# Order of work in a two-layer attention and expert kernel: paired copies and spreads of x's sums, gathered rows turned behind pieces, attention's first units in another order

## The chip, the cores and the metric

The kernel runs on one core of a Trainium2 chip. A core has a matrix engine (TensorE, called PE here; PEld is its weight load), VectorE (DVE), ScalarE (ACT), GpSimd (POOL) and SyncE (SP, which only issues transfers here), each with its own instruction stream in program order. They meet through semaphores. Matrix products go to PSUM, banks of 2 KB on each of 128 partitions; everything else lives in SBUF. The metric is device time in microseconds (us), lower is better.

## The reference

x is 8 batches of 256 tokens with 256 features, in float32. Four blocks follow one another, each added to x:

```python
x = x + L0_xattn(layernorm(x), ctx, ctx)   # autocorrelation attention: one row per batch, added to all tokens
x = x + L0_ffn(layernorm(x))               # 8 experts, each gets exactly 256 tokens
x = x + L1_xattn(layernorm(x), ctx)        # 16 heads of 16, softmax attention
x = x + L1_ffn(layernorm(x))               # top 2 of 8 experts, and a shared one
```

The parts that this change touches are the end of the first block, the second, and the beginning of the third:

```python
# L0_ffn
norm = layer_norm(feat);  scores = norm @ centroids.T
for e in range(8):                       # balanced: each expert takes its best C = 256 of the tokens left
    idx_e = top_k(where(taken, -inf, scores[:, e]), C);  taken[idx_e] = True
routed = feat[idx];  h = layer_norm(routed)
out = routed + gelu(h @ w1 + b1) @ w2 + b2     # per expert, put back in place
# L1_xattn
q = norm(x) @ Wq;  k, v = ctx @ Wkv;  out = softmax(q k / 4) v @ Wp
```

## The kernel before

All of it is one program in which the order of instructions on each engine is written out by hand: an engine runs what is emitted for it in just that order. The function is `fast_path`.

**x's sums (L1848 to L2128).** After the first block each batch b needs x plus a row of its own. `copy_rows(b)` multiplies x of a batch by the identity into a PSUM tile `po`; `spread_rows(b)` adds the batch's row of PB to it, on one of four groups of 32 rows of the array (group b // 2). `order_b` is 0, 2, 4, 6, 1, 3, 5, 7, so neighbours in it lie on different groups. `take(b)` computes mean and variance from `po` on DVE (`tile_stats`, two a batch), copies it back to X on ACT and stores it to NMd in DRAM. For two batches `act_sums` gets the sums on ACT instead, with `squares` behind it. `factors` (rstd by pow on POOL and a Newton step), `widen` and `factor_rows` turn the factors to rows `psr` on PE; `factors_out` copies them to `srow`; `times_factors` multiplies the scores `ps0` (expert 0) and `psx` (all) by them to `n0` and SC. Before that, `pw` and `pb` are small products copied to WCn and `bound`, `pr3` and `pp` give PB, and `pcp` gives cP, which `rows_part` adds to the scores. The PSUM pools are `ps_t` (four banks), `ps_k` (two) and one bank for the tag `pg`.

**The search (L2179 to L2535).** For experts 0 to 6 in turn, `search` finds the score limit in five rounds: DVE counts scores above a trial limit, PE sums the counts (`pcn`, L2210), DVE makes the next trial. While an expert is searched for, the list of the one before is built, a step a round (`list_tokens`: pse, ppl, `pid`, pix, then the gather of its 256 rows from NMd into R, issued by POOL). Between `pcn`s PE runs pieces from a queue called `work`: each piece is one 0.43 us matmul of a longer computation (keys and values of the third block, then the products of the experts). `fill(us)` takes pieces for that many us by their assumed costs. `start_ffn` calls `ffn` for the expert whose rows were gathered; it is called in round r == 1 of a search, after the first search, and in the tail. `ffn` has ACT scale R, PE transpose it at once (`prt`, L2378), ACT copy it to RT (L2382), and puts its products (`ph`, then `py`) at the end of `work`. More than 24 pieces in the queue are run before a new `ffn`:

```python
        if listed:
            while len(work) > 2 * NF + 8:
                work.popleft()[1]()
            ffn(*listed.popleft())
```

**Attention's start (L2544 to L3060).** The experts' results come back from DRAM (Yd) as `yg`; `add_y` adds them to X on DVE. For each batch `batch_stats` (DVE, pow on POOL, a Newton step of four operations on POOL or DVE), `norm_q` (h), `turn_q` (transposes `pt`, L2622) and `queries` (QM, half on ACT, half on DVE) come before its `scores` (`p`, L2669; exponentials on ACT) and `values` (`pv`). Values of the context tiles from EARLY on are pieces of `work`; those before it are computed here by `vals`. The main loop goes over units (batch b, half c of the heads).

Of the kernel before, what the change touches and what calls it, by code (L numbers as in the profile page):

```python
# [1086 lines left out]
def fast_path(  # L1087
# [276 lines left out]
    kmax = pk.tile([P, NB, NTB], F32, name="kmax")  # L1364


    EARLY = 7

    def attention_columns():

# [477 lines left out]
    def rows_of(b):  # L1848
        return X[:, TPB * b : TPB * (b + 1), :]

    def copy_rows(b, pool):
        pos[b] = pool.tile(
            [P, TPB, D], F32, tag="pt" if pool is ps_t else "pm", name="po"
        )
        nc.tensor.matmul(
            pos[b].rearrange("p h d -> p (h d)"),
            ident,
            rows_of(b).rearrange("p h d -> p (h d)"),
            start=True,
            stop=False,  # L1860
            skip_group_check=True,
        )
# [13 lines left out]
            )  # L1876

    for b in order_b[:4]:
        copy_rows(b, ps_t)
    fill(0.87)  # L1880
    WCn = pa.tile([P, 3, 32], F32, name="WCn")
    pw = ps_a.tile([P, 3, 32], F32, tag="pg", name="pw")
    for j in range(3):
        for dc in range(KC):
            nc.tensor.matmul(
# [3 lines left out]
                start=(dc == 0),  # L1889
                stop=(dc == KC - 1),  # L1890
            )
    nc.vector.tensor_copy(WCn, pw)
    bnd = pa.tile([E, 1], F32, name="bnd")
    nc.vector.tensor_scalar(bnd, cs[:, 1:2], 1.01, None, ALU.mult)
    bdiag = pa.tile([E, E], F32, name="bdiag")
    nc.vector.tensor_scalar(bdiag, ident[:E, :E], bnd, None, ALU.mult)
    pb = ps_k.tile([P, E], F32, tag="pm", name="pb")
    nc.tensor.matmul(pb, ones[:E, :], bdiag, start=True, stop=True)
# [39 lines left out]
    pcp = ps_k.tile([P, 32], F32, tag="pm", name="pcp")  # L1938
    for j in range(2):
        nc.tensor.matmul(  # L1940
            pcp, R3[:, j, :], WCn[:, j, :], start=(j == 0), stop=(j == 1)
        )
    PB = pa.tile([P, D], F32, name="PB")
    nc.vector.tensor_tensor(PB, pp, boutb, ALU.add)
    cP = pa.tile([P, 32], F32, name="cP")
    nc.vector.tensor_tensor(cP, pcp, WCn[:, 2, :], ALU.add)

    rm = pa.tile([P, NT, 2], F32, name="rm")
    r2, mr2 = rm[:, :, 0], rm[:, :, 1]
# [12 lines left out]
            )  # L1962


    psr = ps_a.tile([P, 2, TPB, P], F32, tag="pg", name="psr")

    def factor_rows(k):
        for h in range(TPB):
# [58 lines left out]
    def factors(q0, q1, eng):  # L2027
        qs = slice(q0, q1)
        return rstd(MV[:, qs, :], r2[:, qs], 1.0 + LN_EPS, LN_EPS**2, eng, mr2[:, qs])
# [16 lines left out]
        nc.vector.tensor_tensor(dst[:, halves[m]], ps[:, halves[m]], srow[:, m, :], ALU.mult)  # L2046

    def factors_out(m):
        nc.scalar.copy(srow[:, m, :], psr[:, m].rearrange("p h t -> p (h t)"))

    b = order_b
    spread_rows(*b[:4])
    copy_rows(b[4], ps_k)
    squares = act_sums(b[3])
    take(b[:1])
    squares()
    spread_rows(b[4])
    copy_rows(b[5], ps_t)
    spread_rows(b[5])
    take(b[1:2])  # L2060
    squares = act_sums(b[5])
    take(b[2:3])
    newton_a, means_a = factors(0, 8, nc.gpsimd)
    newton_a()
    squares()
    for i in b[6:]:
        copy_rows(i, ps_t)
        spread_rows(i)

    def rows_part(ps, cols):  # L2070

# [12 lines left out]
            )  # L2084

    rows_part(ps0, cP[:, 0:1].to_broadcast([P, 32]))
    take(b[4:5])
    widen(0, 8, nc.scalar)
    newton_2, means_2 = factors(8, 12, nc.gpsimd)
    factor_rows(0)  # L2090
# [15 lines left out]
    means_2()  # L2106
    means_3(nc.gpsimd)
    store_factors(1)
    nc.scalar.copy(sx1, psx[:, halves[1]])
    factors_out(1)  # L2110
    times_factors(n0, ps0, 1)
    nc.gpsimd.tensor_tensor(SC[:, halves[1]], sx1, srow[:, 1, :], ALU.mult)
    next(columns)
    pb1 = ps_t.tile([P, E * NF], F32, tag="pt", name="pb1")
    nc.tensor.transpose(pb1, b1r, ident[: E * NF, : E * NF])
    b1c = pr.tile([P, E, NF], F32, name="b1c")
    nc.vector.tensor_copy(b1c.rearrange("p e f -> p (e f)"), pb1)

# [3 lines left out]
    for r in range(NCT):  # L2122
        psel = ps_t.tile([16, P], F32, tag="pt", name="psel")
        nc.tensor.transpose(psel, a16[:, r, :], ident)
        nc.vector.tensor_copy(rowsel[:, r, :], psel)

    ac.close()
    acp.close()  # L2128
# [223 lines left out]
    def ffn(e, ids, R):  # L2352
# [7 lines left out]
        prt = ps_t.tile([P, KC, NCT, P], F32, tag="pt", name="prt")  # L2360
        for r in range(NCT):
            nc.scalar.activation(
                R[:, r, 0:D],
                R[:, r, 0:D],
                AF.Identity,
                bias=R[:, r, D + 1 :],
                scale=R[:, r, D : D + 1],
            )
            if e in TPART and r == NCT - 1:

                nc.scalar.copy(blank[:, D : D + 1], blank[:, D + 1 : D + 2])
                n0_, n1_ = TPART[e]
                nc.sync.dma_start(
                    out=Td.rearrange("(n p) w -> p n w", p=P)[:, n0_:n1_, :],
                    in_=blank.unsqueeze(1).to_broadcast([P, n1_ - n0_, ROW]),
                )
            for kc in range(KC):
                nc.tensor.transpose(  # L2378
                    prt[:, kc, r, :], R[:, r, kc * P : (kc + 1) * P], ident
                )  # L2380
        for kc in range(KC):
            nc.scalar.activation(  # L2382
                RT[:, kc, :],
                prt[:, kc].rearrange("p r q -> p (r q)"),
                AF.Identity,
                bias=gbc[:, 1, kc : kc + 1],
                scale=gbc[:, 0, kc : kc + 1],
            )

        def up(f):  # L2390
            ph = ps_h.tile([P, CAP], F32, tag="ph", name="ph")
# [160 lines left out]
    py = ct_scope.enter_context(tc.tile_pool(name="py", bufs=2, side="right"))  # L2552
    warm = small.tile([P, 1], F32, tag="warm", name="warm")
    nc.scalar.activation(warm, ones[:, 0:1], AF.Exp)
    ygs = [py.tile([P, NF, D], F32, tag="yg", name="yg") for _ in range(2)]
    for i0, i1 in ((2, 4), (4, 8), (8, 16)):
        nc.sync.dma_start(
            out=ygs[i0 // 8][:, i0 % 8 : (i1 - 1) % 8 + 1, :],
            in_=Yd.rearrange("(c p) d -> p c d", p=P)[:, i0:i1, :],
        )  # L2560

    QM, hTs, h2s, norms = {}, {}, {}, {}

    def add_y(i, n):

        nc.vector.tensor_tensor(
            X[:, i : i + n, :],
            X[:, i : i + n, :],
            ygs[i // 8][:, i % 8 : i % 8 + n, :],
            ALU.add,  # L2570
        )

    def batch_stats(b, tag, eng=nc.gpsimd):

# [400 lines left out]
    for b in range(B):  # L2975
        for c in range(NB):
# [489 lines left out]
```

## Time and profile before

| | |
|---|---|
| median of three runs | 902.32 us (894.98 to 902.54) |
| the profiled execution | 899.05 us, of which the instructions span 897.3 |
| busy in that span | PE 866.9, DVE 307.1, ACT 266.7, POOL 217.3 us |
| sums of x and the start of the search (45 to 67) | PE busy 20.49 of 22 us, DVE 15.61 |
| search (60 to 185) | PE busy 113.60 of 125 us |
| last two experts (185 to 231) | PE busy 42.67 of 46 us |
| start of attention (231 to 262) | PE busy 27.90 of 31 us |
| rest, from 400 on | PE busy 491.71 of 497 us |

Busy is the time in which an engine had at least one instruction running. A wait row of the profile names the instruction that waited, what released it, and how long the engine stood idle for it. The granted clock is the share of PE's full clock that the chip allowed in a stretch; at 0.50 the same matmul takes about twice as long. In a timeline row, "x8" joins eight instructions, and a float32 product here is two of them.

### The profile page before, as it was taken

Reading aid. Unit: us, or ns where it says so; the run is one execution under the profiler, and the core shown is the slowest. Engines: PE = TensorE matmul, PEld = TensorE weight load, DVE = VectorE, ACT = ScalarE, POOL = GpSimd, SP = SyncE. Lnnn points to the kernel's source line nnn. Section 1 sums busy time; section 2 is a strip of 40 time slices with the busy share of each in tenths; the row PEclk is TensorE's granted clock in tenths of the full one; section 3 lists DMA queues with packets and bytes.
Section 4 is the critical chain, followed back from the end, with each engine's and each line's share of the span. In section 5 each row is a group of like instructions: output and inputs, shape, how many; then the busy total and the mean of one; then the engine's idle time right before and its main releaser. Section 6 shows DMA issues by size and latency. Waiting matters only on the chain.

```text
span 897.3 us, 11174 instructions
## 1 busy us (share of the span) xinstructions
PE 866.9 (97%) x4200; PEld 539.0 (60%) x4200; DVE 307.1 (34%) x1016; ACT 266.7 (30%) x499; POOL 217.3 (24%) x302
## 2 busy tenths in 40 slices
PE   8999888989999999999999999999999999999997
PEld 7546677778745555544748565656565556574745
DVE  7377865330445575454112111111111111111011
ACT  4255453224377677431010111111111111111110
POOL 7060221221335554433320011020202131111200
PEclk9999999999999999999999999999999999999999
DMA  7564379642250001081120535555555633311130
GB/s 244 185 201 162 117 218 277 189 136 82 94 141 2 1 1 37 20 312 54 66 68 24 188 100 155 174 154 176 143 186 134 193 88 110 88 12 13 14 104 27
DMA packets 86218, 105.21 MB, mean 117 GB/s; under 512 B 7915, under 2 KB 76748, under 8 KB 86124
## 3 DMA queue, kind: packets, MB, share of 16 engines
q1 hardware_dynamic: 77642, 91.09, 31.7%
q0 software_dynamic: 7920, 13.02, 6.8%
q8 instruction: 35, 0.57, 0.2%
q10 hardware_dynamic: 594, 0.30, 0.1%
q14 instruction: 27, 0.22, 0.1%
HBM read 80.60 MB, written 25.37 MB: 118 GB/s over the span
## 4 chain that ended last, share of the span: by engine, by line
PE 84%; DMA 4%; DVE 3%; issue 3%; POOL 2%; ACT 2%; ACTq 0%; POOLq 0%; DVEq 0%; SPq 0%
PE pgt L3086 19%; PE py L3108 18%; PE pu L3086 18%; PE py L2410 6%; PE ph L2393 4%; PE p L2669 4%; PE pv L2684 3%; DMA R<-NMd,ids 2%; PE pp L2735 2%; PE pp L2636 1%; PE pp L1406 1%; PE pgu L3281 1%; PE pt L2622 1%; DMA C<-in_ctx_dram 1%; PE pt L3142 1%
## 5 line engine op out<-in xcount | busy, mean ns | idle before, releaser
L3095 DVE TENSOR_TENSOR A<-A,pu 128x512 f32<-128x512 f32 x96 | 66.0, 688 | 365.2 <-PE pu L3086 358.5
L3094 ACT ACTIVATE A<-pgt 128x512 f32<-128x512 f32 x96 | 57.4, 598 | 271.4 <-PE pgt L3086 271.4
L3155 POOL DMA_INDIRECT Od<-Y,ids x32 | 49.5, 1546 | 303.5 <-ACT Y L3168 208.6
L3086 PE MATMUL pgt<-RT,wa 128*128 128x512 f32 x256 | 121.1, 595 | 0.0
L3086 PE MATMUL pu<-RT,wb 128*128 128x512 f32 x256 | 120.3, 592 | 0.0
L3108 PE MATMUL py<-wc,A 128*128 128x256 f32 x512 | 111.8, 379 | 0.0
L3108 PEld LDWEIGHTS py<-wc,A 128*128 128x128 f32 x512 | 96.7, 190 | 13.3 <-issue 0.5
L2677 ACT ACTIVATE ex<-p,scale 128x512 f32<-128x512 f32 x128 | 77.5, 691 | 33.7 <-PE p L2669 33.7
L3086 PEld LDWEIGHTS pu<-RT,wb 128*128 128x128 f32 x256 | 48.6, 190 | 61.2 <-issue 60.0
L3086 PEld LDWEIGHTS pgt<-RT,wa 128*128 128x128 f32 x256 | 47.6, 190 | 54.9 <-issue 54.5
L2393 PE MATMUL ph<-RT,w 128*128 128x256 f32 x256 | 63.7, 398 | 0.2 <-ACT A L2402 0.2
L2410 PE MATMUL py<-w,A 128*128 128x256 f32 x256 | 60.3, 385 | 0.0
L2393 PEld LDWEIGHTS ph<-RT,w 128*128 128x128 f32 x256 | 47.7, 198 | 9.4 <-ACT A L2402 1.8
L2402 ACT ACTIVATE A<-ph,b1c 128x256 f32<-128x256 f32 x64 | 30.2, 474 | 75.2 <-PE ph L2393 73.4
L2410 PEld LDWEIGHTS py<-w,A 128*128 128x128 f32 x256 | 47.3, 190 | 6.4
L2909 POOL DMA_INDIRECT Td<-HP,to x32 | 31.6, 988 | 64.6 <-DMA Td<-HP,to 61.5
L3086 PE MATMUL pgt<-HT,wa_-1_2777 128*128 128x512 f32 x96 | 45.5, 596 | 0.0
L3086 PE MATMUL pu<-HT,wb_-1_2778 128*128 128x512 f32 x96 | 45.1, 592 | 0.0
L2669 PE MATMUL p<-QM,KT 32*128 32x512 f32 x256 | 44.6, 651 | 0.4 <-DVE QM L2650 0.4
L3168 ACT ACTIVATE Y<-py,R 128x256 f32<-128x256 f32 x32 | 15.2, 474 | 96.5 <-PE py L3108 96.5
L3108 PE MATMUL py<-wc_-1_2779,A 128*128 128x256 f32 x192 | 41.9, 379 | 0.0
L3108 PEld LDWEIGHTS py<-wc_-1_2779,A 128*128 128x128 f32 x192 | 36.4, 190 | 5.8 <-issue 1.0
(463 smaller groups left out, 1001.6 us busy)
## 6 DMA issues: line engine op xcount, KB each, us to landing
w<-in_L_ffn_w_dram SPq DMA_DIRECT2D x16, 1024.0 KB, 5.6
wa<-in_L_ffn_w_e_dram SPq DMA_DIRECT2D x8, 1024.0 KB, 5.5
wb<-in_L_ffn_w_e_dram SPq DMA_DIRECT2D x8, 1024.0 KB
wc<-in_L_ffn_w_e_dram SPq DMA_DIRECT2D x8, 1024.0 KB
R<-Td SPq DMA_DIRECT2D x8, 530.0 KB
sa<-in_L_ffn_w_e_dram SPq DMA_DIRECT2D x16, 256.0 KB, 3.9
sb<-in_L_ffn_w_e_dram SPq DMA_DIRECT2D x16, 256.0 KB, 6.2
sc<-in_L_ffn_w_e_dram SPq DMA_DIRECT2D x16, 256.0 KB, 2.9
```

The costliest lines, as they stand in the source:

```text
L2393: nc.tensor.matmul(ph, w1[:, kc, f * P : (f + 1) * P], RT[:, kc, :], start=(kc == 0), stop=(kc == KC - 1),)
L2402: nc.scalar.activation(A[:, f, :], ph, AF.Gelu_apprx_tanh, bias=b1c[:, e, f : f + 1])
L2410: nc.tensor.matmul(py, A[:, f, r * P : (r + 1) * P], w2[:, f, :], start=(f == 0), stop=(f == NF - 1),)
L2669: nc.tensor.matmul(ps[g].rearrange("p m q -> p (m q)"), KT[rows, c, k0 : k0 + P], QM[b][rows, c].rearrange("p m q -> p (m q)"), start=True ...
L2677: nc.scalar.activation(e4[:, g], ps[g], AF.Exp, scale=scale)
L2684: nc.tensor.matmul(pvs[b, c][32 * g : 32 * g + 32, m, :], VA[:, b * TPB + kt, 8 * c + 2 * g + m, :], ex[b, c, kt][:, g, m, :], start=(kt = ...
L2909: nc.gpsimd.indirect_dma_start(out=Td, out_offset=bass.IndirectOffsetOnAxis(ap=to[g][:, k, j : j + 1], axis=0), in_=HP[:, GT * g + j, :], ...
L3086: nc.tensor.matmul(ps, w_[:, kc, fs], xs[kc], start=(kc == 0), stop=(kc == KC - 1),)
L3094: nc.scalar.activation(a, pgt, AF.Silu)
L3095: nc.vector.tensor_tensor(a, a, pu, ALU.mult)
L3108: nc.tensor.matmul(py, A[:, f, s : s + P], wc[:, f, :], start=(f == 0), stop=(f == NF - 1))
L3155: nc.gpsimd.indirect_dma_start(out=Od, out_offset=bass.IndirectOffsetOnAxis(ap=ids, axis=0), in_=Y, in_offset=None, compute_op=ALU.add,)
```

## The change

In x's sums, the fifth batch's copy takes the place of two pieces, the last four batches are copied and spread as two pairs, `act_sums` is left to one batch, `pb` shares the bank of `pw` and comes first, `pcp` is computed later, `psr` is allocated at its first use, `srow` is copied ahead of `sx1`, and three small copies go from DVE to ACT:

```diff
-    EARLY = 7
+    EARLY = 6
...
     for b in order_b[:4]:
-        copy_rows(b, ps_t)
-    fill(0.87)
+        copy_rows(b, ps_t, "pt")
+    copy_rows(order_b[4], ps_k, "pm")
+    bnd = pa.tile([E, 1], F32, name="bnd")
+    nc.vector.tensor_scalar(bnd, cs[:, 1:2], 1.01, None, ALU.mult)
+    bdiag = pa.tile([E, E], F32, name="bdiag")
+    nc.vector.tensor_scalar(bdiag, ident[:E, :E], bnd, None, ALU.mult)
     WCn = pa.tile([P, 3, 32], F32, name="WCn")
-    pw = ps_a.tile([P, 3, 32], F32, tag="pg", name="pw")
+    pw = ps_a.tile([P, 4, 32], F32, tag="pg", name="pw")
+    pb = pw[:, 3, 0:E]
+    nc.tensor.matmul(pb, ones[:E, :], bdiag, start=True, stop=True)
...
     spread_rows(*b[:4])
-    copy_rows(b[4], ps_k)
+    copy_rows(b[5], ps_a, "pg")
+    spread_rows(*b[4:6])
     squares = act_sums(b[3])
     take(b[:1])
     squares()
-    spread_rows(b[4])
-    copy_rows(b[5], ps_t)
-    spread_rows(b[5])
     take(b[1:2])
-    squares = act_sums(b[5])
+    pcp = ps_t.tile([P, 32], F32, tag="pt", name="pcp")
+    for j in range(2):
+        nc.tensor.matmul(
+            pcp, R3[:, j, :], WCn[:, j, :], start=(j == 0), stop=(j == 1)
+        )
+    for i in b[6:]:
+        copy_rows(i, ps_t, "pt")
+    spread_rows(*b[6:])
     take(b[2:3])
+    cP = pa.tile([P, 32], F32, name="cP")
+    nc.vector.tensor_tensor(cP, pcp, WCn[:, 2, :], ALU.add)
     newton_a, means_a = factors(0, 8, nc.gpsimd)
     newton_a()
-    squares()
-    for i in b[6:]:
-        copy_rows(i, ps_t)
-        spread_rows(i)
...
-    take(b[4:5])
+    take(b[4:6])
...
+    factors_out(1)
     nc.scalar.copy(sx1, psx[:, halves[1]])
-    factors_out(1)
...
-    nc.vector.tensor_copy(b1c.rearrange("p e f -> p (e f)"), pb1)
+    nc.scalar.copy(b1c.rearrange("p e f -> p (e f)"), pb1)
...
-        nc.vector.tensor_copy(rowsel[:, r, :], psel)
+        nc.scalar.copy(rowsel[:, r, :], psel)
```

In the search, the transposes of an expert's rows and the copy to RT become an entry of `work`, charged 0.5 us, behind up to three entries that are there; and `start_ffn` is called in round 2 instead of 1:

```diff
+        def turn_rows():
+            prt = ps_t.tile([P, KC, NCT, P], F32, tag="pt", name="prt")
+            for r in range(NCT):
+                for kc in range(KC):
+                    nc.tensor.transpose(
+                        prt[:, kc, r, :], R[:, r, kc * P : (kc + 1) * P], ident
+                    )
             for kc in range(KC):
...
+                nc.scalar.activation(
+                    RT[:, kc, :],
...
+        work.insert(min(3, len(work)), (0.5, turn_rows))
...
-            if r == 1 and e >= 2:
+            if r == 2 and e >= 2:
                 start_ffn()
```

At attention's start, Y is loaded batch by batch into two buffers, each load two batches ahead, and added batch by batch; batch 1's Newton step and all of its normalization are DVE's; both halves of batch 0's queries come before the first scores, and the values of tiles 4 and 5 behind them:

```diff
+    def load_y(b):
+        if b < B:
+            ygs[b] = py.tile([P, TPB, D], F32, tag="yg", name="yg")
+            nc.sync.dma_start(
+                out=ygs[b],
+                in_=Yd.rearrange("(c p) d -> p c d", p=P)[:, TPB * b : TPB * (b + 1), :],
+            )
+
+    load_y(1)
+    load_y(2)
...
+    def add_y(b):
+        xb = X[:, TPB * b : TPB * (b + 1), :]
+        nc.vector.tensor_tensor(xb, xb, ygs.pop(b), ALU.add)
+        load_y(b + 2)
...
-    add_y(TPB, TPB)
-    batch_stats(1, "q")
+    add_y(1)
+    batch_stats(1, "q", nc.vector)
     queries(0, 0)
-    norm_q(1, nc.gpsimd, nc.vector)
+    queries(0, 1)
+    norm_q(1, nc.vector, nc.vector)
     add_bias(0)
     add_bias(1)
-    list(vals(4, 1, ps_m))
...
             if prev is None:
-                queries(0, 1)
+                list(vals(4, 1, ps_m, nc.vector.tensor_copy))
                 turn_q(1)
-                add_y(4, 4)
-                list(vals(5, 2, ps_m, nc.vector.tensor_copy))
+                add_y(2)
+                batch_stats(2, "q")
...
-                if b + 2 < B:
+                if b + 2 < B and b:
+                    add_y(b + 2)
                     batch_stats(b + 2, "q")
...
             if prev is None:
-                add_y(8, 4)
-                add_y(12, 4)
+                list(vals(5, 1, ps_m, nc.vector.tensor_copy))
                 ct_scope.close()
```

More of the change, by code (lines that the diff above doesn't have):

```diff
@@ L1849, in rows_of, with copy_rows @@
         return X[:, TPB * b : TPB * (b + 1), :]
[L1851 to L1854, printed above, removed]
+    def copy_rows(b, pool, tag):
+        pos[b] = pool.tile([P, TPB, D], F32, tag=tag, name="po")
         nc.tensor.matmul(
@@ L1891, in fast_path @@
             )
[L1892 to L1898, printed above, removed]
+    nc.vector.tensor_copy(WCn, pw[:, 0:3, :])
     bound = pr.tile([P, E], F32, name="bound")
@@ L1937, in fast_path @@
         nc.tensor.matmul(pp, R3[:, j, :], woutr[:, j, :], start=(j == 0), stop=(j == 1))
[L1938 to L1942, printed above, removed]
     PB = pa.tile([P, D], F32, name="PB")
     nc.vector.tensor_tensor(PB, pp, boutb, ALU.add)
-    cP = pa.tile([P, 32], F32, name="cP")
-    nc.vector.tensor_tensor(cP, pcp, WCn[:, 2, :], ALU.add)
     rm = pa.tile([P, NT, 2], F32, name="rm")
@@ L1962, in store_factors @@
             )
-    psr = ps_a.tile([P, 2, TPB, P], F32, tag="pg", name="psr")
+    psrs = []
     def factor_rows(k):
+        if k == 0:
+            psrs.append(ps_a.tile([P, 2, TPB, P], F32, tag="pg", name="psr"))
+        psr = psrs[0]
         for h in range(TPB):
@@ L2048, in factors_out @@
     def factors_out(m):
-        nc.scalar.copy(srow[:, m, :], psr[:, m].rearrange("p h t -> p (h t)"))
+        nc.scalar.copy(srow[:, m, :], psrs[0][:, m].rearrange("p h t -> p (h t)"))
     b = order_b
     spread_rows(*b[:4])
-    copy_rows(b[4], ps_k)
+    copy_rows(b[5], ps_a, "pg")
+    spread_rows(*b[4:6])
     squares = act_sums(b[3])
@@ L2359, in ffn @@
         Y = pf.tile([P, NCT, D], F32, tag="Y", name="Y")
-        prt = ps_t.tile([P, KC, NCT, P], F32, tag="pt", name="prt")
         for r in range(NCT):
@@ L2376, in ffn @@
                 )
-            for kc in range(KC):
-                nc.tensor.transpose(
-                    prt[:, kc, r, :], R[:, r, kc * P : (kc + 1) * P], ident
-                )
[L2381 to L2388, printed above, removed]
+        def turn_rows():
[5 more added lines that the diff above has]
+                    )
+            for kc in range(KC):
+                nc.scalar.activation(
+                    RT[:, kc, :],
+                    prt[:, kc].rearrange("p r q -> p (r q)"),
+                    AF.Identity,
+                    bias=gbc[:, 1, kc : kc + 1],
+                    scale=gbc[:, 0, kc : kc + 1],
+                )
+        work.insert(min(3, len(work)), (0.5, turn_rows))
         def up(f):
@@ L2551, in fast_path @@
     pq2 = at.enter_context(tc.tile_pool(name="pq2", bufs=2))
-    py = ct_scope.enter_context(tc.tile_pool(name="py", bufs=2, side="right"))
+    py = at.enter_context(tc.tile_pool(name="py", bufs=2))
     warm = small.tile([P, 1], F32, tag="warm", name="warm")
     nc.scalar.activation(warm, ones[:, 0:1], AF.Exp)
[L2555 to L2560, printed above, removed]
-    QM, hTs, h2s, norms = {}, {}, {}, {}
[L2564 to L2571, printed above, removed]
+    ygs = {}
+    def load_y(b):
[7 more added lines that the diff above has]
+    load_y(2)
+    QM, hTs, h2s, norms = {}, {}, {}, {}
+    def add_y(b):
+        xb = X[:, TPB * b : TPB * (b + 1), :]
+        nc.vector.tensor_tensor(xb, xb, ygs.pop(b), ALU.add)
+        load_y(b + 2)
     def batch_stats(b, tag, eng=nc.gpsimd):
```

## The prediction

> **What bounds the kernel.** The page's first part comes first, then the waits of the matrix engine (PE) over the whole span (what waited, on whom: us in total, times, longest).
>
> ```profile
> PE 866.9 (97%) x4200; PEld 539.0 (60%) x4200; DVE 307.1 (34%) x1016; ACT 266.7 (30%) x499; POOL 217.3 (24%) x302
> ...
> PE prt L2378 <- ACT R L2362: 10.0, 9, 2.2
> PE pt L2622 <- POOL h L2598: 1.9, 3, 0.7
> ...
> PE pt L2622 <- DVE h L2598: 1.0, 1, 1.0
> PE pb L1898 <- DVE bdiag L1896: 0.7, 1, 0.7
> ```
>
> PE is busy all but 30 us, and its work is the same in both kernels, so a gain is idle PE time removed or PE time spent badly. A third of the idle is one wait: the transposes of gathered rows (prt) wait for ACT's scaling of R. The timeline shows the worst case and DVE's work beside it, the stage view (us; per engine busy us and instructions; clock; DMA) what followed.
>
> ```profile
> 150.67 0.99 PE L2378 MATMUL prt<-ident,R 128*128 128x128 f32 x3 [2.25 <-ACT R L2362]
> 151.04 0.17 ACT L2371 COPY blank<-blank 128x1 f32<-128x1 f32 x1
> 151.12 0.29 DVE L2294 TENSOR_TENSOR ob<-oab,tok 128x256 f16<-128x256 f16 x1
> ```
>
> ```profile
> 148.00:150.00 2.00, 0.42 (x5) 0.21 (x3) 1.48 (x8) 0.44 (x1) 0.00 (x0) 1.00 1.05 359
> 152.00:154.00 2.00, 2.00 (x6) 1.53 (x6) 0.00 (x0) 1.30 (x3) 0.00 (x0) 0.50 1.02 328
> ```
>
> After 2.25 us idle the clock is 0.50 for some 3.4 us, and PE is "busy" there with 6 matmuls in 2 us instead of some 11. The same stands after the gaps at 186 (2.02 and 0.57 us) and 254 (1.03 and 0.68). The sums of x before the search, PE's part of the timeline:
>
> ```profile
> 43.53 1.99 PE L1869 MATMUL po<-PB,spread 32*128 32x512 f32 x8
> 45.45 1.12 PE L1855 MATMUL po<-X,ident 128*128 128x512 f32 x2
> 46.51 1.12 PE L1869 MATMUL po<-PB,spread 32*128 32x512 f32 x2
> 47.56 1.12 PE L1855 MATMUL po<-X,ident 128*128 128x512 f32 x2
> ```
>
> Eight spread matmuls on four row groups took 1.99 us at the clock of 0.50 granted there (42 to 45); two alone take 1.12 at full clock. DVE's statistics wait up to 1.95 us (at 51.88) for this alternation. Last, the start of attention (timeline):
>
> ```profile
> 239.32 0.54 DVE L2650 TENSOR_SCALAR QM<-pp,mask,bqm 128x256 f32<-128x256 f32 x1
> 239.41 0.69 POOL L2584 TENSOR_TENSOR b_r<-b_ve,powers 128x2 f32<-128x2 f32 x1 [4.59 <-DVE b_ve L2582]
> ...
> 239.92 0.71 PE L2669 MATMUL p<-QM,KT 32*128 32x512 f32 x4 [0.37 <-DVE QM L2650]
> ```
>
> Here DVE is free for QM, since the Newton steps behind pow are POOL's.
>
> **A. Copies and spreads in pairs.** PE's side first. Now there are four copies, two fill pieces, then from 45.45 to 53.88 four copies and four spreads by turns, 1.05 us from start to start. After the change b4's copy (0.86) stands where the two pieces stood (1.03), and spreads go as four, two, two. A pair on two row groups should cost what one costs (four cost 1.99 at half clock, so about 1.0 at full): 2 x 1.05 saved. Copies back to back take 0.86 instead of 1.05: some 0.4 saved. pb goes ahead of pw, with bdiag long ready: 0.7 of wait goes, but the bank is shared, so pr3 now waits for DVE to copy both WCn and bound (0.26 + 0.17) out of it: 0.5 saved net. pcp leaves the shadow of PB (0.9 there) and is paid behind the second spread: 0.6 lost. Sum 2.1 + 0.4 + 0.5 - 0.6 = 2.4. The copies of b6 and b7 need banks of po that are read out by then; three are, the last with ACT's copy of b1 at 48.2 or so, when PE gets there.
>
> DVE's chain: it gets b5 too, 14 statistics of 0.57 us from about 45.0, which end at 53 (before: 55.16); ACT loses b5's sums and squares. POOL's first rstd (51.16 now) no longer stands behind nmean of b5 (50.70) and starts some 2 us sooner. At the end ACT writes srow ahead of sx1 (0.37 long, 0.2 of it on the path), and b1c and rowsel (0.23 + 0.48 on DVE, ahead of the first count at 60.44) go to ACT, which is busy 2.9 of 7 us from 54 to 61 and whose rowsel is wanted by pix, 12 us later; without that cover it would cost about the same 0.7 there. 53 + pow 1.2 + Newton 0.65 + widen 0.3 + psr 0.7 + srow 0.4 + n 0.45 + count 0.75 = 57.5. PE's own order gives 58.0 for the first pcn, now 61.23: 3.2 saved. The two pieces are paid later (0.93): net **-2.3** (ends -1.2 and -2.7). NMd's rows leave in another order on SP, but the first gather is at 74, far behind.
>
> **B. Rows turned behind three pieces, and from r == 2.** Nine waits: 0.50, 1.48, 1.05, 1.05, 2.25, 0.62, 2.02 + 0.57, 0.51 = 10.05. Three pieces are 1.35 us of matmul, and experts 1 to 4 start a round later, 2 to 3 us more. All are covered; for expert 6, which isn't moved to another round, three pieces reach 187.4 while R is ready at 187.9 and 188.9, but the queue is deeper by then (four pieces from the fill and from EARLY = 6, about one for each turn that is charged 0.5), and what is over 24 is run ahead of it: some 2 us. What is late next: pid waits for DVE's ob, which ends 3.1 us after pcn of r = 1 (148.20 to 151.41; the same at 99.87, 114.43 and 131.31), and until now the stalled turn stood in between. With four pieces (1.9 us) search 3 waits 1.2, with six (2.8) searches 4 to 6 wait 0.3 each: 2.1 back. Behind the turn, ph needs RT 1.1 us after prt ends; the pieces left there (nine for expert 1 at r = 1, so some five to nine now; 17 and more for others) hide it, 0.3 taken. Sum -10.05 + 2.1 + 0.3 = **-7.6**.
>
> The clock: 14 ph matmuls took 4.47 us from 189.47 and 10 took 3.73 from 151.67, against 0.22 each: 1.4 and 1.5, with prt 0.3 more: **-3.2**. The Trainium skill ("TensorE: Matmul & The Clock Gate", Why this matters for your kernels) asks only for no idle gap over about 3 us; by it gaps of 2.25 cost no clock and B ends at -7.6. The row shows 0.50 behind 2.25 us, while 1.48 us at 100 left it at 1.00, and I follow the row: -10.8.
>
> **C. Attention's start.** batch_stats(1) now does its Newton steps on DVE ahead of QM: pow starts at 239.4, ends at 240.1, four steps to 240.85, QM to 241.4. PE ends queries(0,1) at 239.6 and waits 1.9 instead of 0.37; all of scores stands behind it. Then vals(4) covers turn_q(1) (0.63 gone), batch 2's statistics come at 246 instead of 250.06, so turn_q(2)'s 1.03 + 0.68 go, and exps are the pace (2.42 each four): scores(1,0) at 254.1 instead of 256.56. The half clock there (eight p matmuls take 1.79 from 256.56 and 1.14 elsewhere, sixteen pv 1.93 and 1.07) is worth 1.5 more. One vals tile of 1.03 left for the fill: -3.9 + 1.03 = -2.9. New idle of 1.9 may draw a slow stretch itself: 0.4 x 1.7 = 0.7. In later batches add_y (0.68 on DVE) stands ahead of the statistics; h of batch 3 is already late by 0.59, batches 5 and 7 have 0.1 and 0.4 to spare: 1.2 (from 0 to 1.6). A rule speaks against it: "SBUF — State Buffer", Who interferes with whom, has a DVE add of two SBUF inputs block POOL's reads. The pow at 251.50, beside such adds, took 1.62 instead of 0.69; by the rule 0.68 more at batches 3 and 5. I keep 1.2 and give the rule to the range. SP waits for each add before the next load of Y, with only shared weights behind it. Net **-1.0** (-3 to +2).
>
> **Sum.** -2.3 - 7.6 - 3.2 - 1.0 = -14.1. The profiled execution spans 897.3 and took 899.05, so 885; the median of the runs is 3.3 above it, 888. The spread of the runs (894.98 to 902.54) may come from the very gaps that go, so I take **886**.
>
> **Rivals.** *Gaps go, the clock stays*: slow stretches come at new gaps (1.9 at 239.6, 1.2 at pid). For: 0.50 followed a stretch with only small matmuls at 38 to 42; against: 1.48 idle drew none. It gives back 3.2 and 1.7: 891. *Waits only move*: gathers land 2.7 to 7.8 us after issue beside weight loads, and DVE's chain, not PE, sets the rounds once the turn's stall is gone; half of B, the clock's part and all of C go: -2.3 - 3.8 = -6, between 893 and 896 by the two bases of the sum: 895. Against: DVE waits 16.4 us in all for pcn. *The queue runs dry* (slower): starting a round later needs pieces for that round. If fewer than four were left at r = 1, PE would stand for the 3.2 us of DVE's chain and 1.8 for RT at four experts, 20 us, with four slow stretches of 1.7: 899 - 3 + 27 = 923. Expert 1 has nine left (18 py matmuls between 102.13 and 107.06), so I give it little.
>
> **Numbers.** Forecast 0.70 (own range 880 to 890), clock stays 0.16, waits move 0.11, dry queue 0.03. The range 878 to 893 leaves out most of the last two and a tail below. Runs of this kernel differ by 0.8%, so about 1% is the least that can be told; faster by that is under 893.3: 0.70 + 0.16 = 0.86, the same 0.11, slower 0.03.
>
> **What would show it.** prt's wait under 1 us; pid waiting for ob some 2 us; clock 1.00 from 60 to 231; first pcn near 58; a wait of about 1.9 of p for QM at the start of attention. A prt that still waits, or ph waiting for RT by more than 1 us, would prove B wrong; a first pcn later than 60, A.

## The result and the profile after

The changed kernel takes 890.34 us (median of nine runs, 885.95 to 894.02), the kernel before 901.34 beside it (894.98 to 910.85). The ratio of the runs is 0.989, with a 95% interval from 0.9857 to 0.9923. The profiled execution of the changed kernel took 893.59 us, of which its instructions span 891.8.

The first row of the page, and then the waits of PE over the span (what waited, on whom: us in total, times, longest):

```profile
PE 864.1 (97%) x4200; PEld 539.3 (60%) x4200; DVE 309.2 (35%) x1026; ACT 265.3 (30%) x495; POOL 213.6 (24%) x294
```

```profile
PE pid L2295 <- DVE ob L2291: 3.3, 5, 1.2
PE p L2673 <- DVE QM L2654: 2.9, 1, 2.9
PE pse L2253 <- DVE sel L2248: 2.2, 4, 0.8
PE ph L2395 <- ACT A L2404: 2.1, 3, 1.1
PE pt L2626 <- POOL h L2602: 1.6, 2, 1.3
```

The wait that headed the list before, prt for ACT's scaling with 10.0 us, is gone from it. In its place stand pid for ob (1.2 before), ph for A (0.2 before) and, at the start of attention, p for QM (0.4 before), which is longer than anything that was forecast there.

PE's part of the timeline through the sums of x (start us, us, engine, line, operation, idle before it) and the same stretch by the clock's windows (us; per engine busy us and instructions in the order PE, PEld, DVE, ACT, POOL; granted clock; share of DMA; GB/s):

```profile
44.11 2.09 PE L1867 MATMUL po<-PB,spread 32*128 32x512 f32 x8 [0.52 <-DVE PB L1937]
46.13 2.08 PE L1853 MATMUL po<-X,ident 128*128 128x512 f32 x2
48.13 2.08 PE L1867 MATMUL po<-PB,spread 32*128 32x512 f32 x4
...
54.22 1.13 PE L1867 MATMUL po<-PB,spread 32*128 32x512 f32 x4
```

```profile
40.00:43.40 3.40, 2.82 (x9) 1.82 (x8) 0.82 (x3) 0.00 (x0) 0.00 (x0) 0.50 1.08 371
...
50.20:53.60 3.40, 3.40 (x9) 1.97 (x8) 2.20 (x9) 0.73 (x2) 2.26 (x5) 0.50 0.73 163
53.60:57.00 3.40, 3.40 (x34) 0.98 (x36) 1.51 (x6) 1.31 (x3) 1.21 (x2) 0.99 0.44 154
```

The pair at 54.22, at full clock, costs what one spread cost before. But the pair at 48.13 took 2.08, and one copy at 46.13 as much: here the clock stood at 0.50 for 13.7 us, from 40.0 to 53.7 (3.4 us before the change). That is why the first pcn comes at 62.47 us in this execution, later than before (61.24), though PE has less to do until then.

Cut at three marks (the first pcn; pbp, a small product that opens attention's part; and the first pgt, a product of the last block's experts), the two profiled executions compare as follows. The search and the last experts are all of part B, attention is part C. The before column has a half clock of 3.4 us in the first row, two in the second and one in the third; the after column has 13.7 us in the first and 3.4 in the third.

| stretch, us | before | after |
|---|---|---|
| start to the first pcn | 61.24 | 62.47 |
| first pcn to pbp (search, last experts) | 170.86 | 161.87 |
| pbp to the first pgt (attention) | 136.9 | 139.0 |
| first pgt to the end | 528.3 | 528.4 |

### The profile page after: what moved, and what is told of

It reads as the page before. It is cut to its first block, busy times and chain, and to the rows that moved or that the text cites. A ratio compares the mean times of both kernels' runs of the same rounds, so it can differ in the third digit from the quotient of the medians.

```text
span 891.8 us, 11183 instructions
## 1 busy us (share of the span) xinstructions
PE 864.1 (97%) x4200; PEld 539.3 (60%) x4200; DVE 309.2 (35%) x1026; ACT 265.3 (30%) x495; POOL 213.6 (24%) x294
## 4 chain that ended last, share of the span: by engine, by line
PE 85%; DMA 5%; DVE 5%; POOL 1%; SPq 1%; issue 1%; ACT 1%; ACTq 0%; DVEq 0%; POOLq 0%
PE pgt L3090 19%; PE py L3112 19%; PE pu L3090 18%; PE ph L2395 4%; PE py L2412 4%; PE p L2673 4%; PE pv L2688 3%; DMA Td<-blank 2%; PE pp L2739 2%; PE pp L2640 2%; PE pp L1427 1%; PE po L1853 1%; DMA row<-SCd 1%; PE pgu L3285 1%; PE pt L3146 1%
## 5 line engine op out<-in xcount | busy, mean ns | idle before, releaser
L2395 PE MATMUL ph<-RT,w 128*128 128x256 f32 x256 | 61.6, 387 | 2.1 <-ACT A L2404 2.1
L2395 PEld LDWEIGHTS ph<-RT,w 128*128 128x128 f32 x256 | 45.4, 189 | 10.3 <-ACT A L2404 4.0
```

Source lines behind the costliest of these rows:

```text
L2395: nc.tensor.matmul(ph, w1[:, kc, f * P : (f + 1) * P], RT[:, kc, :], start=(kc == 0), stop=(kc == KC - 1),)
```

## A second measure: the span at full clock

A single execution hides how much of its time is the clock's doing. Each execution comes with its span and its mean granted clock. From these follows its half-clock time, (1 - clock) x time x 2, less a flat 4 us for the tail behind the last matmul, where the records show 0.50 too (for 2 to 6 us, some of it behind the span); no difference below depends on that constant. It explains most of the differences between executions of one kernel: for before (49 executions), part A (20), part B (5), part C (12) and the changed kernel (9), straight lines give 0.38 to 0.42 us of span for each us at half clock, with correlations from 0.98 to 1.00. With 0.41 for all, taken back to no half-clock time, they give the **span at full clock** used below: 893.5 us before, 885.1 after. It is good to about half a us for these five and to 1 or 2 for kernels with four executions. The median half-clock time fell from 14 to 8.5 us, worth some 2 us. So of the gain about 8.4 us is order of work and about 2 is clock.

## The experiments

**Each part alone.** Three kernels, each the kernel before with one part of the change.

```diff
 part A alone
+    copy_rows(order_b[4], ps_k, "pm")
...
+    copy_rows(b[5], ps_a, "pg")
+    spread_rows(*b[4:6])
```

> The kernel before with part A alone (x's sums: pairs, pb with pw, pcp later, srow ahead of sx1, three copies on ACT). Theory 1: the waits and the thinner matmuls of A hold the clock at 0.50 for about 13.7 us from 40, as in the changed kernel, and eat its gain: first pcn near 62.5 (before 61.2), later stages as before, whole kernel within 2 us of before. Rival: the long slow stretch was chance; then it is 3.4 us here, first pcn comes near 58, and the kernel is 2 to 3 us faster than before.

Measured: 897.24 us median (893.41 to 904.46, 20 runs), ratio 0.9957 (0.9926 to 0.9988), span at full clock 891.3, which is 2.2 below before. In the profiled execution there was no half clock at 40 us, and the first pcn came at 56.48. So the pairs do gain what they should, and the 13.7 us at half clock don't come with part A each time; part B alone, which follows, has more of them without A. Part C alone, whose sums of x are those of before, had no half clock there either and its first pcn at 59.88, so at an equal clock A brings it 3.4 us forward.

```diff
 part B alone
+        work.insert(min(3, len(work)), (0.5, turn_rows))
...
-            if r == 1 and e >= 2:
+            if r == 2 and e >= 2:
```

> The kernel before with part B alone (rows turned behind three pieces, start_ffn in round 2). Theory 1: B carries the whole gain: prt waits for nothing, pid waits for ob about 2.3 us in all, no slow clock between 60 and 230, and from first pcn to pbp 159 to 160 us instead of 170.9; the kernel is about 11 us faster than before. Rival: part of the stage's gain came with A's earlier and deeper queue; then prt or ph still waits 2 to 3 us and the gain is 7 to 8.

Measured: 890.82 us (888.68 to 899.46, 5 runs), ratio 0.9894 (0.9868 to 0.992), span at full clock 884.7: 8.8 below before. The profiled execution has even 27.3 us at half clock from 39.9 on, with the sums of x as they were before. From the first pcn to pbp it takes 162.3 us, against 170.9. Its waits of PE:

```profile
PE pid L2298 <- DVE ob L2294: 3.6, 6, 1.2
PE pse L2256 <- DVE sel L2251: 2.8, 5, 0.8
PE prt L2381 <- ACT R L2361: 2.3, 2, 1.9
```

Here prt still waits at the last two experts, while ph waits only 0.2 us for A; in the changed kernel it is the other way round. The gain lies between the 11 us of the theory and the 7 to 8 of the rival, and the rival was right about the wait: the deeper queue that covers the last of it comes with EARLY = 6, which is tested as part of C. Parts A and B without it (further down) still have 1.7 us of prt.

```diff
 part C alone
-    EARLY = 7
+    EARLY = 6
...
+    batch_stats(1, "q", nc.vector)
     queries(0, 0)
-    norm_q(1, nc.gpsimd, nc.vector)
+    queries(0, 1)
+    norm_q(1, nc.vector, nc.vector)
```

> The kernel before with part C alone (EARLY = 6, attention's first units, rows added batch by batch). Theory 1: C costs: p waits 2.9 us for QM, a slow stretch follows, and from pbp to the first pgt it takes 139 us instead of 136.9, while one more vals tile (1.0) lies ahead: the kernel is 2 to 3 us slower than before. Rival: C is neutral by itself and lost only by what A and B did to the clock's phase; then that stage takes 136 to 137 and the kernel is within 1 us.

Measured: 901.75 us (897.95 to 913.25, 12 runs), ratio 1.0015 (0.9996 to 1.0034), span at full clock 895.6: 2.1 above before. p waits 2.9 us for QM here too. The ratio alone can't tell the two kernels apart; the span at full clock can, and by it part C costs time.

**Which of C's edits costs it.** First, the changed kernel with batch 1's Newton steps back on POOL:

```diff
-    batch_stats(1, "q", nc.vector)
+    batch_stats(1, "q")
```

> The changed kernel with batch 1's Newton step on POOL again, so that QM does not stand behind pow on DVE. Theory 1 (queue order on DVE): p's wait for QM falls from 2.9 to under 0.5 us, no slow stretch at 230 to 240, the stage from pbp to the first pgt 135 to 136 us instead of 139: 3 to 4 us faster than the changed kernel. Rival: turn_q(1) waits for h then, since POOL does the Newton step beside add_bias, and gives most of it back: the stage still takes 138 or more.

Measured: 889.05 us (886.04 to 891.53, 4 runs), ratio 0.9876 (0.984 to 0.9913). The wait of p is 0.4 us, and pbp to the first pgt takes 135.5 us instead of 139.0. Some 1.0 of the 139.0 is a half clock, as will be seen; at an equal clock the gain is 2.5. The span at full clock is 882.1, good to 1 or 2, against 885.1. The place of these four small operations in DVE's order is what makes p wait.

But the forecast had that order in it and expected 1.9 us, not 2.9. DVE's part of the timeline of the changed kernel at that place, then POOL's:

```profile
227.10 0.16 DVE L2593 TENSOR_TENSOR b_t<-b_r,b_ve 128x2 f32<-128x2 f32 x1 [0.85 <-POOL b_r L2588]
...
232.39 1.22 DVE L2593 TENSOR_TENSOR b_t<-b_r,b_ve 128x2 f32<-128x2 f32 x1 [0.81 <-POOL b_r L2588]
```

```profile
231.66 0.69 POOL L2588 TENSOR_TENSOR b_r<-b_ve,powers 128x2 f32<-128x2 f32 x1 [4.60 <-DVE b_ve L2586]
232.33 1.25 POOL L2618 TENSOR_TENSOR X<-X,bpb 128x512 f32<-128x512 f32 x1
```

The same operation on two columns takes 0.16 us for batch 0 and 1.22 for batch 1, where it starts 0.06 after POOL's addition of the bias and ends 0.03 after it. Two kernels ask whether the one holds up the other. The first writes the additions later in the program:

```diff
     norm_q(1, nc.vector, nc.vector)
-    add_bias(0)
-    add_bias(1)
...
                 turn_q(1)
+                add_bias(0)
+                add_bias(1)
                 add_y(2)
```

> The changed kernel with the additions of the bias to x for batches 0 and 1 (POOL, 1.25 us each) moved behind the turn of batch 1's queries; Newton stays on VectorE. Theory (VectorE's first Newton operation took 1.22 us instead of 0.16 because POOL was adding beside it): it is 0.2 us or less, p waits 1.9 us for QM instead of 2.9 as the prediction had it, and the stretch from pbp to the first pgt is 1.0 us shorter than the changed kernel's 139.0. Rival (the 1.22 us are the operation's wait for POOL's table of powers, not contention): the operation stays at about 1.2 us and the wait at 2.9.

Measured: 888.14 us (886.38 to 889.94, 4 runs), ratio 0.9862 (0.9813 to 0.9912). It looked like a win for the rival, with the operation at 1.22 and the wait at 2.9, but it tested nothing: POOL has nothing else in its queue between the power and the addition, so the addition ran at the same moment. What it did give is this stretch without a half clock behind the wait: 138.0 us from pbp to the first pgt, 1.0 less than in the changed kernel's profile, where eight p matmuls took 2.09 us instead of 1.14. The second kernel puts the additions behind an operation of POOL that comes later:

```diff
                 add_y(2)
                 batch_stats(2, "q")
+                add_bias(0)
+                add_bias(1)
```

> The changed kernel with the additions of the bias to x for batches 0 and 1 put behind the statistics of batch 2 in POOL's own queue, so that they can't start before POOL's power for batch 2 (in e6 they were written later but POOL had nothing else before them, and they ran at the same moment). Newton stays on VectorE. Theory (POOL's addition held up VectorE's first Newton operation, 1.22 us instead of 0.16): it takes 0.2 us or less, p waits about 1.9 us for QM instead of 2.9, and pbp to the first pgt is about 1 us shorter than e6's 138.0. Rival (the 1.22 us are not contention with the addition): the operation stays at 1.2 us and the wait at 2.9.

Measured: 890.64 us (883.85 to 892.82, 4 runs), ratio 0.9821 (0.9736 to 0.9905), span at full clock 884.3, 0.8 below the changed kernel's. Its median is no better because three of its four executions had 10 us or more at half clock. DVE's part of the timeline, and PE's wait:

```profile
231.23 0.16 DVE L2593 TENSOR_TENSOR b_t<-b_r,b_ve 128x2 f32<-128x2 f32 x1 [0.81 <-POOL b_r L2588]
231.42 0.16 DVE L2594 TENSOR_TENSOR b_t<-b_t,b_r 128x2 f32<-128x2 f32 x1
```

```profile
PE p L2673 <- DVE QM L2654: 1.9, 1, 1.9
```

0.16 us, a wait of 1.9, and 137.0 us from pbp to the first pgt, 1.1 less than with the additions at the old moment. So contention between DVE and POOL made the missing 1.0 us.

**The change without C.** Parts A and B on the kernel before:

```diff
+    spread_rows(*b[4:6])
...
+        work.insert(min(3, len(work)), (0.5, turn_rows))
...
     batch_stats(1, "q")
     queries(0, 0)
     norm_q(1, nc.gpsimd, nc.vector)
```

> Before with parts A and B only (sums in pairs, turn behind pieces), attention's start as before. Theory (C costs 1.9 us, as in e3): 888 us median, 2 us under the changed kernel at the same clock; p waits 0.4 us for QM and pbp to the first pgt is 136.5 to 137. Rival (C earns its place together with A and B, because the half clock at attention's start comes only there): equal to the changed kernel or slower, 890 to 892 us.

Measured: 886.81 us (883.87 to 893.88, 4 runs), ratio 0.9879 (0.9797 to 0.9961), span at full clock 883.0, good to 1.5. The runs can't tell it from the changed kernel; the stages can: pbp to the first pgt takes 136.3 us, 1.8 less than the changed kernel's order takes without a half clock (138.0). It does so although one vals tile more (1.03 us) is computed there, so that C's order costs some 2.8 us of PE's time in attention at an equal clock. In this profiled execution the clock is full throughout, and the first pcn comes at 57.08.

**The new waits of ph.** Two of ph's waits for A are long, 0.88 us at 151.76 and 1.07 at 183.72. At the first, ACT stands in the scaling of R while ph needs its A: at 149.60 it waits 0.75 us for the second gather, and the copy behind it 0.94 for a transfer. The scaling is moved behind two pieces and the turn behind five (with the Newton steps on POOL):

```diff
-        for r in range(NCT):
+        def scale_rows():
+            for r in range(NCT):
...
-        work.insert(min(3, len(work)), (0.5, turn_rows))
+        work.insert(min(2, len(work)), (0.0, scale_rows))
+        work.insert(min(5, len(work)), (0.5, turn_rows))
```

> e4 with the scaling of the gathered rows (ScalarE) moved behind two more pieces and the turn behind five instead of three. Theory (two of the new ph waits for ACT, 0.9 and 1.1 us, are ScalarE standing in the scaling, which waits for the second gather and for the copy's DMA): ph's waits for A fall from 2.1 us to under 0.5, none of them goes to prt, and the time from the first pcn to pbp falls from 161.9 to 160 us; median 1.5 to 2 us under e4. Rival (the wait only moves: the turn then waits for the scaled rows, or RT for ACT): prt's waits for ACT come back with 1 to 2 us, no gain.

Measured: 885.8 us (884.68 to 890.0, 4 runs), ratio 0.9854 (0.9794 to 0.9913). ph's wait is gone from the list, as it is in the one other kernel with the scaling behind (e11, below). With the scaling ahead it has between 0.6 and 2.1 us in five executions of the same search (2.1 changed, 1.8 e4, 1.4 e6, 0.8 e9, 0.6 e10). So the order on ACT bears on the wait, but what sets its size is not shown, and at 183.72 the scaling stands behind the A that ph waits for, not ahead of it. First pcn to pbp takes 161.3 us, against 161.5 with the scaling ahead, a difference that says nothing: e9 and e10, with the same search as the changed kernel, take 160.6, the changed kernel 161.9. The groups of instructions by line show where it went, first for the kernel with only the Newton steps moved, then for this one:

```profile
L2378 PE MATMUL prt<-ident,R 128*128 128x128 f32 x32 | 4.8, 273 | 0.0
```

```profile
L2379 PE MATMUL prt<-ident,R 128*128 128x128 f32 x32 | 6.5, 291 | 0.6 <-ACT R L2359 0.4
```

The turn takes 1.7 us more and waits 0.6: at most experts PE stands for some 0.2 us between the transposes of the first and of the second half of R (the third of four starts 0.3 us after the second instead of 0.11), and the row counts most of that as busy. No gain shows: as the rival had it, the wait moved, if by less than its 1 to 2 us.

**The half clock at 40 us.** The narrow products (pw, pr, pp) stand behind the copies there. In seven of the ten profiled executions with that order the clock fell near 40 us (before, changed, B alone, e4, e6, e8, e9), for 3.4 to 27.3 us, in three it didn't (A alone, C alone, e7). Two ways to give PE more in that stretch. The first, on the kernel with the Newton steps on POOL, repeats 256 columns of one copy three times:

```diff
+            nc.tensor.matmul(
+                pos[b0][:, 0, :],
+                ident,
+                X[:, TPB * b0, :],
+                start=True,
+                stop=False,
```

> The changed kernel with batch 1's Newton steps on POOL (as in e4) and three more copies of 256 columns of one batch of x, put into the thin stretch before the pairs (after WCn's products, before pp and after pp); they write the same values again and cost about 1.3 us of PE if nothing idles there. Theory (the slow stretch at 40 us is set off by PE being busy too little of the time in the thin stretch, with narrow products and short waits): no slow stretch at 40 us, first pcn at 57 to 58 us instead of 62.5, every execution's mean clock 0.995 or more, median 884 to 886 us. Rival (it is set off by something else, such as how much PE had done by then, or by chance): the stretch at 40 us comes with 13 us at half clock as in the changed kernel and in e4, and the median is that of e4 or 1 us more, 889 to 890 us.

Measured: 3611.61 us (3549.9 to 3641.68, 4 runs), so its time says nothing: behind the fast path the kernel ran its general branch as well (1024 pgt matmuls of another function), which it does when its own tests of the routing fail. The repeated product changes the sums. "PSUM — Partial Sum Buffer" of the Trainium skill, The four PSUM rules, says that a product that starts a group clears the written marks of the whole 2 KB bank, whatever part it writes, and that the next accumulating product then overwrites there. By that the spread replaces x in the other 256 columns. It fits, and no run here separates it. Up to attention the trace can still be read: the clock is full in every window from 33 to 57 us, and the first pcn comes at 57.40. This is one execution, and three of ten did without a half clock there anyway, so it agrees with the theory and proves nothing.

The second, on the changed kernel, adds nothing but holds three of the five early copies back:

```diff
-    for b in order_b[:4]:
+    for b in order_b[:2]:
         copy_rows(b, ps_t, "pt")
-    copy_rows(order_b[4], ps_k, "pm")
...
     nc.vector.tensor_copy(WCn, pw[:, 0:3, :])
+    copy_rows(order_b[2], ps_t, "pt")
...
     nc.vector.tensor_scalar(R3, pr3, rtot, None, ALU.mult)
+    copy_rows(order_b[3], ps_t, "pt")
...
     nc.vector.tensor_tensor(PB, pp, boutb, ALU.add)
+    copy_rows(order_b[4], ps_k, "pm")
```

> The changed kernel with three of the five early copies of x held back: one behind WCn's products, one behind the products for R, one behind pp; the same work in another order. Theory (the half clock at 40 us follows a stretch in which PE does only narrow products with three waits of 0.5 us): the waits before pr, pp and the first spread (0.47, 0.58, 0.52 us) are covered, no half clock between 36 and 54 us, first pcn at 55.5 to 56.5 us instead of 62.5, median 1.5 us under the changed kernel's time at a full clock, 884 to 886 us. Rival (the half clock comes there whatever PE does, with the transfers that begin there, say, or with what the chip drew before): the first pcn comes at 60 us or later, with a stretch at half clock near 40 us; gain 1.5 us at most.

Measured: 886.97 us (886.09 to 888.13, 4 runs), ratio 0.9798 (0.972 to 0.9876). A half clock still came at 38.1 in the profiled execution, but lasted 3.4 us, and the first pcn came at 57.04. At full clock it gains nothing: its best execution took 886.09, the changed kernel's 885.95. Then the same on the kernel with the Newton steps on POOL and the later scaling:

```diff
     nc.vector.tensor_scalar(R3, pr3, rtot, None, ALU.mult)
+    copy_rows(order_b[3], ps_t, "pt")
...
-    batch_stats(1, "q", nc.vector)
+    batch_stats(1, "q")
```

> e8 (Newton on POOL, scaling and turn later) with the copies held back as in e10. Theory: what e10 gains is added to e8: 883 to 884 us median, little spread between executions. Rival (the half clock stays): 885 to 886 us, as e8.

Measured: 884.83 us (883.3 to 887.63, 6 runs), ratio 0.9777 (0.9717 to 0.9837), the fastest median of all. PE's part of its timeline:

```profile
38.06 1.13 PE L1924 MATMUL pr<-vT,CW 128*128 128x128 f32 x8 [0.82 <-DMA CW<-Wd]
39.03 1.02 PE L1853 MATMUL po<-X,ident 128*128 128x512 f32 x2
39.89 1.03 PE L1936 MATMUL pp<-woutr,R 128*128 128x256 f32 x4
40.75 1.02 PE L1853 MATMUL po<-X,ident 128*128 128x512 f32 x2
41.70 1.14 PE L1867 MATMUL po<-PB,spread 32*128 32x512 f32 x8
```

Two of the three waits (pp for R, the first spread for PB) are covered, the third turned into one for a transfer: pr now comes before its operand does. Of the ten executions with held copies nine had a mean clock of at least 0.997; of the 29 executions of the changed kernel and of its variants with the old order of the copies (e4, e6, e7, e8, e9) six had. The chip is no rival here: all ten ran on one chip, and of the 15 executions of before and of e9 on that same chip one had. So the order of the copies does bear on the half clock. What it is in that order that keeps the clock up, the covered waits or something else, is not separated.

## Why the prediction was right, and where it was off

The forecast was 886 us with a range from 878 to 893, for the change in the direction of faster by over 1%; it came to 890.3. As a ratio, 0.982 was forecast and 0.989 measured. Most of the mechanism was right, and 4.3 us of size were not. The number lies just outside the inner range of 880 to 890, nearest to the rival of 891 in which the gaps go and the clock stays. That rival's mechanism came in part only: the half clocks of the search did go, and one came at the new wait of p, but most of what the clock took came at 40 us, where the rival had named no gap. The other two rivals are out: part B alone gained 8.8 us, not half of 7.6, and no wait shows a queue that runs dry.

**A was sized rightly.** -2.3 was forecast, -2.2 measured at full clock. The first pcn was forecast at 58.0 and comes at 57.08 where the clock is full. The bound "later than 60 would prove A wrong" was met by the profile (62.47) for a reason outside A: it should have been set at an equal clock.

**B was right in its steps.** -7.6 was forecast without the clock, -8.8 measured, good to half a us. In the whole change prt's wait went from 10.0 us to none (to 2.3 with B alone), and pid's for ob rose by 2.1, just the sum that was forecast for it: the new ones are 1.2 in search 3 and 0.3 to 0.4 in each of searches 4 to 6, one of which the profile puts down to oab. Two terms were not foreseen, and they cancel. ph now waits 2.1 for A. And the turn itself is shorter, because part of its old stall had been counted as busy. The group of the turn before the change and after:

```profile
L2378 PE MATMUL prt<-ident,R 128*128 128x128 f32 x32 | 7.5, 318 | 10.4 <-ACT R L2362 10.0
```

```profile
L2378 PE MATMUL prt<-ident,R 128*128 128x128 f32 x32 | 4.8, 273 | 0.0
```

The same 32 transposes are busy for 2.7 us less. Before, PE stood between those of the first half of R and those of the second: for the first expert the third of four starts 0.33 us after the second (82.26 after 81.93), where it now starts 0.11 after it, and only 0.06 of that is listed as idle. Some 0.5 of the 2.7 is the clock: four transposes at 0.50 took 0.42 to 0.48 us instead of 0.27 to 0.33. The sum of the stretch closes with it: from the first pcn to pbp PE's idle time fell from 14.0 to 8.7 us, the busy time of prt by 2.7, of ph by 2.1 (clock), of py by 0.6, while nine more matmuls of keys and values add 2.0: together -8.7, and the stretch is 9.0 shorter.

**B's clock was right where it was named.** The two half clocks at 151 and 188 are gone with the idle time ahead of them; no window between 60 and 231 is below 0.99. The weighing of the row against the rule of the Trainium skill ("TensorE: Matmul & The Clock Gate", Why this matters for your kernels: no idle gap over about 3 us) thus came out for the row: a half clock followed waits of 2.25 and 2.02 us, and no profiled execution with part B in it has one between 75 and 220 us. Not every such wait draws one: in part A alone the clock stayed full behind 1.84 us at 146.64 and fell behind 2.23 at 184.85.

**The clock as a whole was mis-sized.** The forecast took off -3.2 in the search and 1.5 at attention, gave 0.7 back there, and then hoped for less spread. In the search it was about right (2.1 of ph, 0.5 of prt, up to 0.6 of py). But in the profiled executions most half-clock time lies in the stretch at 40 us, which the change did not relieve; in the median the gain by the clock was some 2 us, not 4, and of the 2 us hoped for from less spread none is left. The forecast had even seen the half clock at 42 to 45, and used it to scale the price of a spread only.

**C is the step that failed.** -1.0 was forecast with two clock terms in it (-1.5 and +0.7), so -0.2 without; +2.1 was measured alone at full clock. Three terms were wrong. The wait of p for QM was 2.9 instead of 1.9. The rule of "SBUF — State Buffer" of the Trainium skill, Who interferes with whom, was weighed for DVE's additions in POOL's way, but by it the one that issues first blocks the other, and here it acted the other way round: POOL's addition had begun 0.06 us earlier and DVE's operation with two SBUF inputs stood until it ended. The half clock behind that wait, entered with a weight of 0.4, came in the profiled execution, with 1.0 us. And add_y ahead of the statistics was sized 1.2 for the later batches; behind the first units PE's gaps over 0.1 us add up to 3.9 us in the changed kernel and to 1.4 without C, 2.5 more. Two lines of DVE and one of PE show how:

```profile
258.18 0.68 DVE L2574 TENSOR_TENSOR X<-X,yg 128x512 f32<-128x512 f32 x1
258.90 0.43 DVE L2583 BATCH_NORM_STATS2 b_st<-X 128x6 f32<-128x256 f32 x1
...
264.79 0.55 PE L2626 MATMUL pt<-ident,h 128*128 128x128 f32 x3 [1.32 <-POOL h L2602]
```

The addition stands ahead of the statistics, and h of batch 3 comes 1.32 us late instead of 0.58 without C. The same addition at 274.43 and at 306.42 stands ahead of what two tiles of the gates need (gwT and lT), and PE waits 0.75 and 0.79 for them instead of 0.11 and nothing. The 1.0 of QM and the 1.3 that add_y cost above its forecast are the whole difference between -0.2 and +2.1. With the Newton steps left on POOL, C no longer costs: 135.5 us from pbp to the first pgt against 136.3 without it. But a vals tile of 1.03 us lies ahead of that stretch then, so that no gain is left, and by the span at full clock (882.1 against 883.0) the two can't be told apart. That the sum stayed in the range owes something to B, which gave 1.2 us more than forecast and so hid half of what C lost.

## What to carry to other kernels

Compare executions at an equal clock, by span against mean clock, before a stage is judged; a stall of 2 us in a busy engine can cost 1.4 us more in the clock behind it (3.41 us at half clock, at 0.41 each). When small operations move to an engine ahead of something that others wait for, look at what the neighbouring engine does in that very moment, and count the wait for its whole instruction. And a line that is moved in the program moves nothing in time if its engine has nothing else to do: to delay an operation, put it behind one that comes late in the same queue.

## What the runs showed of the hardware

- The clock goes in stretches of 3.41 us. Of the profiled executions' windows in which PE was busy for half or less (0.19 to 0.50), nine of ten were followed by a window at 0.50; the exception had 0.45. Of two with 0.51 and 0.54 the second was. With 0.56 or more it happened only between 35 and 71 us, where many of the products are narrow. So where a stall falls matters: the 2.9 us of p fell into one window in the changed kernel (busy 0.19, the next at 0.50) and across two in e6 (0.58 and 0.56, the next at 1.00), which no order of work decides. The low clock lasted one window nearly everywhere, but one, two, four or eight near 40 us and two at 57 us in e6, in B alone with PE busy throughout the last seven of the eight. What keeps it low there stays open.
- A VectorE operation with two inputs of 128 x 2 elements in SBUF took 1.22 us instead of 0.16 beside a GpSimd addition of 1.25 that had begun 0.06 us earlier.
- Two spreads on two row groups take 1.13 us at full clock, as one does; four on four groups 1.14.
